# Pass 1 of a Mamba block planned with other durations, with a third x_proj tile and the last batch's splits on VectorE

## The chip, the cores and the metric

The kernel runs on one core of a Trainium2 chip. The metric is the device time of one execution in microseconds, lower is better. A core has five instruction streams that run beside each other and wait for each other by semaphores: TensorE (PE: matmuls and transposes, into PSUM), VectorE (DVE), ScalarE (ACT), GpSimd (POOL) and SyncE (SP), which here issues nearly all DMAs. Each stream runs in the order in which its instructions were written.

## The reference

The input is 8 images of 64 x 64 pixels with 96 channels. The part that matters for this case is the first layer's projections; after them come a selective scan, and an attention and a quantized feed-forward layer.

```python
xz = einsum('bhwc,ec->bhwe', groupnorm(x), in_proj_w)       # 96 -> 2 x 192
xin, z = split(xz, 2)
xc = silu(depthwise_conv3x3(xin) + conv_b)                  # 192 channels, 64 x 64
xs = stack([xc by rows, xc by columns, both reversed])      # 4 directions
x_dbl = einsum('bkdl,kcd->bkcl', xs, x_proj_weight)         # 192 -> 6 + 16 + 16
dts, Bs, Cs = split(x_dbl)
delta = softplus(dts @ dt_projs_w + bias)
h = h * exp(delta * A) + delta * u * Bs ;  y = sum_n(h * Cs)   # scan over 4096 positions, 16 states
```

Everything is computed in float32 accuracy. Bs and dts are later multiplied on TensorE in bfloat16, so each float32 value is split into three bfloat16 values that add up to it.

## The kernel before

There are three passes, one after the other, with scratch tensors in DRAM between them. `pass1` makes u (the convolved channels, in both orders), z, the x_proj result and its splits. `pass2` is the selective scan, in 192 pieces of 1024 positions. `pass3` does the rest. Passes 2 and 3 aren't edited.

**Pass 1's units of work.** Batches go in pairs. The 192 channels of a pair of batches are held as three chunks of 128 partitions: chunk 0 (128 channels of the first batch), chunk 1 (128 of the second) and chunk 2 (the other 64 of both). A batch is cut into eight groups of 512 positions. The kinds of unit are:

- `statistics(b, q)`: SP loads 512 positions of x, PE transposes them (four 128-wide transposes into a `pt` tile), VectorE takes `bn_stats`.
- `group_norm(b)`: a few tiny instructions on VectorE, PE (results `pm` and `pv`) and GpSimd give mean and inverse deviation.
- `projection(b, q)`: load and transpose again, normalize on VectorE (`xn`), three matmuls of in_proj (tiles `pa`), copied or passed through SiLU by ScalarE, z stored.
- `convolution(pair, c)`: nine taps on VectorE over 128 x 4096 elements into a tile `u`; then ScalarE applies SiLU in four pieces for the transposed order (`ut`, stored) and in two halves in place.
- `x_projection(b, o, q)`: two matmuls into a tile `px`, evicted to an SBUF tile `xd` by ScalarE (for odd q of the last pair by VectorE) and stored to `xd_d`. It needs the SiLU of chunk 2 and of the batch's own chunk to be done.
- `split(b, o, ...)`: once all eight `xd` of a batch and an order o are stored, SP loads rows of them as `bq`; ScalarE casts to bfloat16, a subtraction leaves the rest, ScalarE casts that, another subtraction gives the third part, and SP stores `bs` to `b_d` or `dt_d`. There are three of these for each batch and order, 48 in all, each with two casts and two subtractions.

**What sets the order.** The units are Python generators. Before an instruction is written, a unit yields the engine it wants, the duration it is planned with, optionally a delay after it (0.3 us if none is given), and optionally a counter of PSUM tiles (`Slots`) that must be free. `weave` keeps a planned clock for each engine and always lets the unit go on that can begin first; ties go by the order of kinds in `room`, which also limits how many units of a kind are open. So the durations in the yields take no time themselves: they decide in what order the instructions stand in each engine's stream, and on SP in what order DMAs are issued. `InOrder` keeps that order as it is written. If an instruction is reached before what it waits for is ready, all behind it on its engine wait too.

**Tiles that are shared.** [...] `p1tr` 2 tiles, `p1mm` 3, `p1px` 2 and `p1ps` 1 (for `pm` and `pv`). `xd`, `bq` and `bs` have three buffers each, `xn` and the loads of projections four.

Every line of pass 1 goes through the recording helper at line 89, which is why the profile names that line throughout; instructions are told apart by their tiles.

Of the kernel before, what the change touches and what calls it, by code (L numbers as in the profile page):

```python
# [33 lines left out]
F32 = mybir.dt.float32  # L34
# [8 lines left out]
P = 128  # L43
# [189 lines left out]
def pass1(ctx, tc, g, consts, ident, mhalf, engines, u_d, z_d, xd_d, b_d, dt_d):  # L233
# [8 lines left out]
    four = ctx.enter_context(tc.tile_pool(name="p1four", bufs=4))  # L242
    ps_tr = ctx.enter_context(tc.tile_pool(name="p1tr", bufs=2, space=PSUM))
    ps_mm = ctx.enter_context(tc.tile_pool(name="p1mm", bufs=3, space=PSUM))
    ps_px = ctx.enter_context(tc.tile_pool(name="p1px", bufs=2, space=PSUM))
    ps_one = ctx.enter_context(tc.tile_pool(name="p1ps", bufs=1, space=PSUM))
    Q = GRP // P

    ORDER = (0, 2, 1)
# [31 lines left out]
        pool.memset(t[:, 1 : HH + 1, WW + 1 : WW + 2], 0.0)  # L281

    sts, gms, us, done = {}, {}, {}, {}
    pts, mms, pxs = Slots(2), Slots(3), Slots(2)
    counts = {}

    def one_more(key, of, end):
# [14 lines left out]
    def statistics(b, q):  # L302
        if b > 1:
            yield "proj", b - 2
        yield "sp", 0.5, 2.0
        x = transposed(three, "xs", b, q)
        next(x)
        yield "pe", 0.7, 0.3, pts
        pt, slot = next(x), pts.taken
        end = yield "dve", 0.7  # L310
        if b not in sts:
            sts[b] = two.tile([C, NG, 6], F32, name="st")
        dve.bn_stats(sts[b][:, q, :], pt[0:C, :])
        pts.release(slot, end)
        one_more(("st", b), NG, end)

    def group_norm(b):

        yield "st", b
        yield "dve", 0.2  # L320
        mv = two.tile([C, 2], F32, name="mv")
        dve.bn_aggr(mv, sts[b].rearrange("p a b -> p (a b)"))
        yield "pe", 0.3
        pm = ps_one.tile([P, 2], F32, name="pm", tag="pm")
        pe.matmul(pm[0:C, 0:1], gmat, mv[:, 0:1], start=True, stop=True)
        yield "dve", 0.5
        gm = wp.tile([C, 2], F32, name=f"gm{b}")
        dve.tensor_copy(gm[:, 0:1], pm[0:C, 0:1])
        dq = two.tile([C, 1], F32, name="dq")
        dve.tensor_sub(dq, mv[:, 0:1], gm[:, 0:1])  # L330
        dve.scalar_tensor_tensor(dq, dq, dq, mv[:, 1:2], ALU.mult, ALU.add)
        yield "pe", 0.3
        pv = ps_one.tile([P, 2], F32, name="pv", tag="pm")
        pe.matmul(pv[0:C, 0:1], gmat, dq, start=True, stop=True)
        yield "dve", 0.2
        dve.tensor_copy(gm[:, 1:2], pv[0:C, 0:1])
        end = yield "pool", 1.0
        pool.tensor_scalar(gm[:, 1:2], gm[:, 1:2], 1e-5, None, ALU.add)
        pool.tensor_tensor(gm[:, 1:2], gm[:, 1:2], mhalf[0:C, 0:1], ALU.pow)
        gms[b] = gm  # L340
        done["stats", b] = end

    def projection(b, q):

        pair, j = b // 2, b % 2
        cols = slice(q * GRP, (q + 1) * GRP)
        rows = slice(1 + q * RPG, 1 + (q + 1) * RPG)
        inner = slice(1, WW + 1)
        own, other = slice(64 * j, 64 * j + 64), slice(64 - 64 * j, P - 64 * j)
        third = xpad[2 + pair % 2]  # L350
        yield "stats", b
        yield "sp", 0.5, 2.0
        x = transposed(four, "xt", b, q)
        next(x)
        if pair > 0:
            yield "conv", pair - 1, j
        if pair > 1:
            yield "conv", pair - 2, 2
        yield "pe", 0.7, 0.3, pts
        pt, slot = next(x), pts.taken  # L360
        end = yield "dve", 0.7
        pts.release(slot, end)
        xn = four.tile([C, GRP], F32, name="xn")
        dve.tensor_scalar(xn, pt[0:C, :], gms[b][:, 0:1], gms[b][:, 1:2], ALU.subtract, ALU.mult)
        def product(w):
            yield "pe", 1.1, 0.3, mms
            p = ps_mm.tile([P, GRP], F32, name="pa", tag="mm")
            pe.matmul(p, w, xn, start=True, stop=True)
            return p, mms.taken

        pa, slot = yield from product(w_in[:, 0:P])
        end = yield "act", 0.6
        act.copy(xpad[j][:, rows, inner], pa.rearrange("p (h w) -> p h w", w=WW))
        mms.release(slot, end)
        pa, slot = yield from product(w_mix[:, j, :])
        yield "act", 0.6
        act.copy(third[own, rows, inner], pa[own, :].rearrange("p (h w) -> p h w", w=WW))
        z1 = three.tile([P, GRP], F32, name="z1")
        end = yield "act", 0.6
        act.activation(z1[other, :], pa[other, :], AF.Silu)  # L380
        one_more(("proj", b), NG, end)
        mms.release(slot, end)
        pa, slot = yield from product(w_in[:, DI : DI + P])
        z0 = three.tile([P, GRP], F32, name="z0")
        end = yield "act", 0.6
        act.activation(z0, pa, AF.Silu)
        mms.release(slot, end)
        yield "sp", 0.9
        sp.dma_start(z_d[b][P:DI, cols], z1[other, :])
        sp.dma_start(z_d[b][0:P, cols], z0)  # L390

    def convolution(pair, c):

        ty = c // 2
        src = xpad[c + pair % 2 if c == 2 else c]
        for b in [2 * pair, 2 * pair + 1] if c == 2 else [2 * pair + c]:
            yield "proj", b
        before = {0: (pair - 1, 1), 2: (pair, 0), 1: (pair, 2)}[c]
        at = 3 * pair + ORDER.index(c) - UB
        if at >= 0:  # L400
            old, c_old = at // 3, ORDER[at % 3]
            for b in {0: (2 * old,), 1: (2 * old + 1,), 2: (2 * old, 2 * old + 1)}[c_old]:
                yield "xproj", b
            yield "stored", old, c_old
        if before[0] >= 0:
            yield "conv", *before
        u = None
        for tap in range(9):
            end = yield "dve", 2.6 if tap == 0 else 4.4, 0.0
            if tap == 0:  # L410
                u = us_p.tile([P, L], F32, name="u")
                us[pair, c] = u
                uv = u.rearrange("p (h w) -> p h w", w=WW)
            win = src[:, tap // 3 : tap // 3 + HH, tap % 3 : tap % 3 + WW]
            if tap == 0:
                dve.tensor_scalar(uv, win, conv_w[:, ty, tap : tap + 1], None, ALU.mult)
            else:
                dve.scalar_tensor_tensor(uv, win, conv_w[:, ty, tap : tap + 1], uv, ALU.mult, ALU.add)
        done["conv", pair, c] = end
        if before[0] >= 0:  # L420
            yield "stored", *before
        parts = chunk_rows(pair, c)
        for w in (slice(i, i + WW // 4) for i in range(0, WW, WW // 4)):
            yield "act", 1.2
            ut = two.tile([P, L // 4], F32, name="ut")
            act.activation(ut.rearrange("p (w h) -> p h w", h=HH), uv[:, :, w], AF.Silu, bias=conv_b[:, ty, :])
            yield "sp", 0.5
            for part, b, ch in parts:
                sp.dma_start(u_d[b][1][ch, w.start * HH : w.stop * HH], ut[part, :])
        for h in range(2):  # L430
            cols = slice(h * (L // 2), (h + 1) * (L // 2))
            end = yield "act", 1.9
            act.activation(u[:, cols], u[:, cols], AF.Silu, bias=conv_b[:, ty, :])
        done["u", pair, c] = end
        end = yield "sp", 0.5
        for part, b, ch in parts:
            sp.dma_start(u_d[b][0][ch, :], u[part, :])
        done["stored", pair, c] = end

    def x_projection(b, o, q):  # L440
# [3 lines left out]
        yield "u", pair, 2  # L444
        px = None
        for ty, u, part in ((0, us[pair, j], slice(0, P)), (1, us[pair, 2], half)):
            end = yield ("pe", 0.85) if px else ("pe", 0.85, 0.3, pxs)
            if px is None:
                px, slot = ps_px.tile([P, GRP], F32, name="px", tag="px"), pxs.taken
            if o == 0:  # L450
# [4 lines left out]
        one_more(("xproj", b), 2 * NG, end)  # L455
        by_dve = pair == NB // 2 - 1 and q % 2 == 1
        end = yield ("dve" if by_dve else "act"), 0.6
        xd = three.tile([2 * NXD, GRP], F32, name="xd")
        (dve.tensor_copy if by_dve else act.copy)(xd, px[0 : 2 * NXD, :])
        pxs.release(slot, end)  # L460
        end = yield "sp", 0.5, 2.5
        sp.dma_start(xd_d[b][o][:, q * GRP : (q + 1) * GRP], xd)
        one_more(("xd", b, o), NG, end)

    def split(b, o, row, rows, pieces, at, dst):

        wide, used = GRP, rows * pieces
        yield "xd", b, o
        yield "sp", 0.5, 2.5
        bq = three.tile([P, wide], F32, name="bq")  # L470
        src = xd_d[b][o][row : row + rows].rearrange("r (s t) -> (r s) t", s=pieces)
        sp.dma_start(bq[0:used], src[:, at : at + wide])
        yield "act", 0.6
        bs = three.tile([P, NS, wide], BF16, name="bs")
        act.copy(bs[0:used, 0, :], bq[0:used])
        yield "pool", 1.2
        pool.tensor_sub(bq[0:used], bq[0:used], bs[0:used, 0, :])
        yield "act", 0.6
        act.copy(bs[0:used, 1, :], bq[0:used])
        yield "pool", 1.2  # L480
        pool.tensor_sub(bs[0:used, 2, :], bq[0:used], bs[0:used, 1, :])
        yield "sp", 0.9
        half = used // 2
        for k2 in range(2):
# [612 lines left out]
```

## Time and profile before

The three timed runs took 10697.7, 10700.71 and 10703.4 us; the profiled execution has a span of 10692.9 us (its run 10694.64 us).

| | busy us of the whole span | busy us in the first 1000 us |
|---|---|---|
| PE matmuls | 7776.9 | 723.2 |
| VectorE | 9619.3 | 595.8 |
| ScalarE | 9298.7 | 429.5 |
| GpSimd | 9181.8 | 259.8 |

The first pass's last split is stored at 954 us of the span, and the second pass's first matmul begins at 975 us. Groups of the first pass in the trace:

| instruction | count | mean |
|---|---|---|
| VectorE conv tap, 128 x 4096 | 96 | 4.59 us |
| PE px record, 128 x 76, 512 columns (a matmul is two records) | 256 | 0.944 us |
| PE pa record, 96 x 128, 512 columns (two to a matmul) | 256 | 0.712 us |
| GpSimd subtraction `bq<-bq,bs`, 128 x 512 | 32 | 2.36 us |
| ScalarE cast `bs<-bq`, 128 x 512 | 64 | 0.618 us |
| ScalarE SiLU piece `ut`, 128 x 1024 | 48 | 2.08 us |
| ScalarE copy `xd<-px`, 76 x 512 | 112 | 0.583 us |

How to read the lines shown below: in the list of waits, "A <- B: total, times, longest" says that engine and tile A stood idle until B was done. In the timeline a line has start, duration (or the stretch of several merged instructions), engine, operation, out<-in tiles, shape, count, and in brackets the idle time of that engine before it and what ended it. "SPq" is SP issuing DMAs.

### The profile page before, as it was taken

To read this page: it belongs to the slowest core of one execution; us is meant where nothing else is said; L and a number is where in the kernel's file an instruction comes from. 1 tells how busy PE (TensorE), PEld (TensorE's weight loads), DVE (VectorE), ACT (ScalarE), POOL (GpSimd) and SP (SyncE) were. 2 spreads that over 40 slices of the span, in tenths; PEclk is the share of its full clock that TensorE was granted. 3 is DMA by queue.
4 is the path that set the end of the run, shared out by engine and by line. 5 is a ranking of instruction groups with operands and counts; after the bars stand their busy time and mean duration, and the time that the engine had idled before them with its cause. 6 is when DMAs were issued, how large, how long until landed. Compare 5 with 4: busy or idle time off the path is not lost.

```text
span 10692.9 us, 151366 instructions
## 1 busy us (share of the span) xinstructions
PE 7776.9 (73%) x51232; PEld 6178.1 (58%) x51232; DVE 9619.3 (90%) x6982; ACT 9298.7 (87%) x21355; POOL 9181.8 (86%) x3270
## 2 busy tenths in 40 slices
PE   6876777777767777777777777777777777766887
PEld 3222656666656666665656666665565666655766
DVE  6664999999999999999999999999999999997776
ACT  4445999999999999999999999999999999996665
POOL 1324999999999999999999999999999999997886
PEclk8777999998899999999899999988999999897776
DMA  5555666669896666689976766789766667997442
GB/s 145 170 165 168 211 217 216 210 211 204 197 210 215 210 219 213 213 205 203 200 218 210 222 211 214 208 200 204 216 210 215 217 207 214 199 198 184 135 128 59
DMA packets 928009, 2103.22 MB, mean 197 GB/s; under 512 B 274391, under 2 KB 422648, under 8 KB 925700
## 3 DMA queue, kind: packets, MB, share of 16 engines
q1 hardware_dynamic: 919812, 2092.79, 69.6%
q8 instruction: 410, 6.72, 0.3%
q14 instruction: 363, 2.97, 0.1%
q10 hardware_dynamic: 7424, 0.74, 0.1%
HBM read 1917.59 MB, written 175.66 MB: 196 GB/s over the span
## 4 chain that ended last, share of the span: by engine, by line
ACT 28%; DVE 20%; PE 17%; issue 17%; POOL 13%; DMA 4%; SPq 1%; ACTq 0%; DVEq 0%; POOLq 0%
DVE h L89 15%; ACT x L89 13%; ACT da L89 10%; POOL c L89 9%; PE wide L89 6%; PE acc L89 6%; DVE wide L89 3%; PE px L89 2%; PE mm L89 2%; ACT L89 1%; POOL xg L89 1%; PE pa L89 1%; ACT delta L89 1%; DMA xdt<-dt_d 1%; SPq L89 1%
## 5 line engine op out<-in xcount | busy, mean ns | idle before, releaser
L89 POOL TENSOR_TENSOR c<-c,h 128x2048 f32<-128x2048 f32 x1536 | 6965.6, 4549 | 395.8 <-DVE h L89 335.4
L89 DVE TENSOR_TENSOR_SCAN h<-da,carry,wide 128x1024 f32<-128x1024 f32 x2304 | 5253.5, 2331 | 204.4 <-PE wide L89 147.4
L89 ACT ACTIVATE x<-duT,bT 128x128 f32<-128x128 f32 (+1 forms) x14336 | 4155.2, 366 | 63.5 <-PE wide L89 57.5
L89 PE MATMUL acc<-ident,c 128*128 128x128 f32 x24576 | 3480.5, 297 | 546.6 <-POOL c L89 539.6
L89 ACT ACTIVATE da<-delta,a_neg 128x1024 f32<-128x1024 f32 x3072 | 3504.2, 1144 | 345.6 <-DVE h L89 333.9
L89 PEld LDWEIGHTS acc<-ident,c 128*128 128x128 f32 x24576 | 3133.3, 155 | 881.1 <-POOL c L89 747.9
L89 PE MATMUL wide<-ident,x 128*128 128x128 f32 x11264 | 1614.0, 292 | 877.9 <-DVE h L89 861.0
L89 PEld LDWEIGHTS wide<-ident,x 128*128 128x128 f32 x11264 | 1344.9, 149 | 1171.7 <-DVE h L89 509.3
L89 DVE TENSOR_TENSOR_SCAN h<-da,wide 128x1024 f32<-128x1024 f32 x768 | 1707.0, 2270 | 82.8 <-PE wide L89 62.0
L89 DVE TENSOR_TENSOR wide<-du,wide 128x1024 f32<-128x1024 f32 x1216 | 1459.2, 1212 | 156.9 <-PE wide L89 156.8
L89 PE MATMUL wide<-xb,sel 96*128 96x512 bf16 x2432 | 752.4, 394 | 584.9 <-DVE h L89 494.7
L89 POOL TENSOR_TENSOR xg<-duT,bT 128x512 f32<-128x512 f32 (+1 forms) x640 | 891.4, 1408 | 82.3 <-PE wide L89 65.1
L89 PE MATMUL wide<-ident,xg 128*128 128x128 f32 x3584 | 500.2, 285 | 239.6 <-DVE h L89 233.7
L89 PEld LDWEIGHTS <-sel 96*128 96x128 bf16 x2432 | 223.0, 101 | 776.0 <-DVE h L89 387.3
L89 PEld LDWEIGHTS wide<-ident,xg 128*128 128x128 f32 x3584 | 412.6, 146 | 316.0 <-issue 143.9
L89 POOL TENSOR_TENSOR du<-delta,u 128x1024 f32<-128x1024 f32 x192 | 455.0, 2370 | 101.4 <-ACT delta L89 92.2
L89 ACT ACT_TABLE_LOAD x385 | 494.0, 1283 | 6.8
L89 PE MATMUL px<-u,w_xp 128*76 128x512 f32 (+1 forms) x512 | 409.5, 929 | 76.5 <-ACT xd L89 47.8
L89 POOL TENSOR_TENSOR bq<-bq,bs 128x512 f32<-128x512 f32 (+1 forms) x48 | 114.2, 2392 | 401.3 <-ACT bs L89 401.2
L89 DVE SCALAR_TENSOR_TENSOR u<-xpad,conv_w,u 128x4096 f32<-128x4096 f32 x96 | 440.6, 4590 | 1.2
L89 PEld LDWEIGHTS px<-u,w_xp 128*76 128x76 f32 (+1 forms) x512 | 78.8, 190 | 364.4 <-issue 217.2
L89 ACT COPY xd<-px 76x512 f32<-76x512 f32 x112 | 65.2, 583 | 254.8 <-PE px L89 169.9
(130 smaller groups left out, 6224.0 us busy)
## 6 DMA issues: line engine op xcount, KB each, us to landing
c<-xd_d SPq DMA_DIRECT2D x1024, 1024.0 KB
c<-xd_d SPq DMA_DIRECT2D x1024, 512.0 KB
u<-u_d SPq DMA_DIRECT2D x128, 512.0 KB
xdt<-dt_d SPq DMA_DIRECT2D x1152, 36.0 KB
xb<-b_d SPq DMA_DIRECT2D x384, 96.0 KB
u<-u_d SPq DMA_DIRECT2D x128, 256.0 KB
y_d<-y SPq DMA_DIRECT2D x24, 1024.0 KB
y<-y_d SPq DMA_DIRECT2D x64, 384.0 KB
```

Source lines behind the costliest of these rows:

```text
L89: ins = getattr(self.engine, op)(*args, **kwargs).ins
```

## The change

Durations and delays in the yields are replaced in many places: x loads (0.5 with 2.0 to 0.6 with 4.0), `pa` products (1.1 to 0.75, delay 0.3 to 0.4), SiLU pieces (1.2 to 2.1), x_proj matmuls (0.85 to 0.9, delay to 0.4), xd stores (0.5 with 2.5 to 0.9 with 3.0), `bq` loads (0.5 with 2.5 to 0.7 with 4.0), and the subtractions of `split`, planned at 1.2 before and now at 4.4 for batches 0 to 5 and 2.5 for batch 6. For batch 7 the subtractions are given to VectorE and planned at 0.65. x_proj gets a third PSUM tile and a fourth `xd` buffer. The bank comes from `pm` and `pv`, which now take tiles of the projections' pool and wait for a free one. Counting the built instructions, only the twelve subtractions of batch 7 change engine; the order changes on all five streams within pass 1, and passes 2 and 3 keep theirs.

```diff
-    ps_px = ctx.enter_context(tc.tile_pool(name="p1px", bufs=2, space=PSUM))
-    ps_one = ctx.enter_context(tc.tile_pool(name="p1ps", bufs=1, space=PSUM))
+    ps_px = ctx.enter_context(tc.tile_pool(name="p1px", bufs=3, space=PSUM))
...
-    pts, mms, pxs = Slots(2), Slots(3), Slots(2)
+    pts, mms, pxs = Slots(2), Slots(3), Slots(3)
...
-        yield "sp", 0.5, 2.0
+        yield "sp", 0.6, 4.0
...
-        yield "pe", 0.3
-        pm = ps_one.tile([P, 2], F32, name="pm", tag="pm")
+        yield "pe", 0.3, 0.3, mms
+        pm, slot = ps_mm.tile([P, GRP], F32, name="pm", tag="mm"), mms.taken
         pe.matmul(pm[0:C, 0:1], gmat, mv[:, 0:1], start=True, stop=True)
-        yield "dve", 0.5
+        end = yield "dve", 0.5
+        mms.release(slot, end)
...
-        end = yield "dve", 0.7
+        end = yield "dve", 0.8
...
-            yield "pe", 1.1, 0.3, mms
+            yield "pe", 0.75, 0.4, mms
...
-            yield "act", 1.2
+            yield "act", 2.1
...
-            end = yield "act", 1.9
+            end = yield "act", 2.0
...
-            end = yield ("pe", 0.85) if px else ("pe", 0.85, 0.3, pxs)
+            end = yield ("pe", 0.9, 0.4) if px else ("pe", 0.9, 0.4, pxs)
...
-        xd = three.tile([2 * NXD, GRP], F32, name="xd")
+        xd = four.tile([2 * NXD, GRP], F32, name="xd")
...
-        end = yield "sp", 0.5, 2.5
+        end = yield "sp", 0.9, 3.0
...
+        name, cost, by = ("dve", 0.65, dve) if b == NB - 1 else ("pool", 4.4 if b < NB - 2 else 2.5, pool)
         yield "xd", b, o
-        yield "sp", 0.5, 2.5
+        yield "sp", 0.7, 4.0
...
-        yield "pool", 1.2
-        pool.tensor_sub(bq[0:used], bq[0:used], bs[0:used, 0, :])
+        yield name, cost
+        by.tensor_sub(bq[0:used], bq[0:used], bs[0:used, 0, :])
         yield "act", 0.6
         act.copy(bs[0:used, 1, :], bq[0:used])
-        yield "pool", 1.2
-        pool.tensor_sub(bs[0:used, 2, :], bq[0:used], bs[0:used, 1, :])
+        yield name, cost
+        by.tensor_sub(bs[0:used, 2, :], bq[0:used], bs[0:used, 1, :])
```

More of the change, by code (lines that the diff above doesn't have):

```diff
@@ L331, in group_norm @@
         dve.scalar_tensor_tensor(dq, dq, dq, mv[:, 1:2], ALU.mult, ALU.add)
-        yield "pe", 0.3
-        pv = ps_one.tile([P, 2], F32, name="pv", tag="pm")
+        yield "pe", 0.3, 0.3, mms
+        pv, slot = ps_mm.tile([P, GRP], F32, name="pv", tag="mm"), mms.taken
         pe.matmul(pv[0:C, 0:1], gmat, dq, start=True, stop=True)
-        yield "dve", 0.2
+        end = yield "dve", 0.2
+        mms.release(slot, end)
         dve.tensor_copy(gm[:, 1:2], pv[0:C, 0:1])
@@ L351, in projection @@
         yield "stats", b
-        yield "sp", 0.5, 2.0
+        yield "sp", 0.6, 4.0
         x = transposed(four, "xt", b, q)
```

## The prediction

> **What bounds the kernel now.** I read the busy share by slice first. Slices 5 to 36 stand at 9 for VectorE, ScalarE and GpSimd (the second pass); only the first four slices are loose. I then split the first 1000 us into windows of 40 us (columns: stretch, length, busy us with instructions of PE, weight loads, VectorE, ScalarE, GpSimd, then granted PE clock, DMA share, GB/s).
>
> ```profile
> DVE  6664999999999999999999999999999999997776
> PEclk8777999998899999999899999988999999897776
> ...
> 400.00:440.00 40.00, 29.54 (x35) 6.14 (x34) 39.68 (x13) 9.97 (x16) 30.86 (x7) 0.55 0.43 111
> 440.00:480.00 40.00, 37.11 (x46) 8.05 (x45) 9.19 (x5) 12.37 (x17) 13.04 (x8) 0.50 0.43 128
> 480.00:520.00 40.00, 24.49 (x55) 10.51 (x53) 28.48 (x11) 24.33 (x34) 13.94 (x6) 0.76 0.63 203
> 640.00:680.00 40.00, 32.11 (x34) 5.56 (x34) 17.01 (x4) 9.49 (x17) 24.92 (x10) 0.50 0.32 90
> 800.00:840.00 40.00, 13.06 (x17) 2.79 (x16) 19.12 (x5) 16.37 (x14) 15.19 (x6) 0.57 0.59 153
> ```
>
> The first pass ends near 954 us (last split stored); PE begins the second pass at 974.96. In 440-480 VectorE worked 9 us of 40 and PE 37, at half clock; in 800-840 nobody worked half of the time. So no engine bounds the first pass as a whole: orders written out by the planner make engines wait in turn. Next the waits over 0-960 (who, for whom: us, times, longest):
>
> ```profile
> DVE xn L89 <- PE pt L89: 156.0, 32, 31.1
> PEld px L89 <- ACT xd L89: 92.5, 42, 9.8
> ACT bs L89 <- DMA bq<-xd_d: 55.3, 18, 9.7
> ACT bs L89 <- POOL bq L89: 52.7, 19, 8.7
> PE px L89 <- ACT xd L89: 47.8, 14, 9.0
> ACT xd L89 <- DMA xd_d<-xd: 45.8, 10, 8.1
> ...
> SPq L89 <- POOL bs L89: 100.2, 18, 14.4
> ```
>
> Read upward: SP stands 100 us in front of stores of `bs` that GpSimd has not made; xd stores queue behind; ScalarE can't evict px or is stuck in a cast; PE waits for px; VectorE waits for the transposes behind px. The timeline shows one whole instance, batches 3 and 4:
>
> ```profile
> 614.22 0.58 ACT L89 COPY xd<-px 76x512 f32<-76x512 f32 x1 [3.25 <-PE px L89]
> 630.66 1.76 ACT L89 CAST bs<-bq 128x512 bf16<-128x512 f32 x3 [9.73 <-DMA bq<-xd_d]
> 632.95 7.73 PE L89 MATMUL px<-u,w_xp 128*76 128x512 f32 x8 [8.95 <-ACT xd L89]
> 639.08 0.62 ACT L89 CAST bs<-bq 128x512 bf16<-128x512 f32 x1 [4.20 <-POOL bq L89]
> 644.30 13.80 POOL L89 TENSOR_TENSOR bs<-bq,bs 128x512 bf16<-128x512 f32 x3
> 645.52 15.40 PE L89 MATMUL px<-u,w_xp 128*76 128x512 f32 x16 [4.83 <-ACT xd L89]
> 663.98 23.07 PE L89 MATMUL px<-u,w_xp 128*76 128x512 f32 x24 [3.06 <-ACT xd L89]
> 688.18 1.59 DVE L89 TENSOR_SCALAR xn<-pt,gm 96x512 f32<-96x512 f32 x2 [31.10 <-PE pt L89]
> ```
>
> One float32 px matmul is two records: 24 records in 23.07 us are 12 matmuls of 1.92 us. VectorE lost 31.1 us at 688 because projection 7's transposes stand behind all of batch 4's px. The same shape, with 30.8 us, ends at 476 (batch 2).
>
> [...] a GpSimd split subtraction takes 1.15 us with VectorE idle (945 us) and 5.33 beside taps (705 us). The old plan charged 1.2 for all. [...] The pools take 2+3+2+1 before and 2+3+3 after; no run here shows a limit. [...] px matmuls are issued without a gap from 664 to 687 and the clock stays 0.50. I don't count on a faster clock. [...] the trace has no such VectorE row (nearest: the xd copy, 0.687).
>
> **The change part by part.** Per-engine work is the same but for 12 subtractions; what moves is the order on every queue of the first pass. Passes two and three keep theirs, and SP's list at the seam (last bq loads, two c loads, last stores, xdt) is the same. So I follow the order from stretch to stretch.
>
> *Batch 2, from the last px of batch 1 (401.7) to projection 5's first transposes (476): 74 us.* Before, statistics of batch 6 preceded conv (pair 1, chunk 1); now its 8 transposes and `bn_stats` lie between the taps. PE sheds 8 x 0.9 = 7 us ahead of batch 1's end. But px of batch 2 now follow those transposes, which come at the pace of taps: about four pairs of tap and two statistics, 4 x (4.47+1.4) = 24 us. Projection 5's transposes stand ahead of 5 of the 32 px matmuls, so 27 x 1.72 (half clock, 46 us) precede them: 24+46 = 70 instead of 74. With the 7 us: 11. The waits for ScalarE inside the old stretch (6.28+4.18+2.77 = 13.2) are in this sum. Beside projection 5 PE was busy 24.5 of 40 us, so the 5 moved matmuls (9 us) fit; the cast wait behind GpSimd near 490 (4.5) goes. Take -15.
>
> *Batch 4, from 614.2 to 688: 74 us.* The new ScalarE order puts two first casts of batch 3's last splits ahead of the last two SiLU pieces of conv (2,2), which px needs. They wait for the store and bq load: cast at 630.66 before; some 10 us after the last px now, as no xd stores of batch 4 are ahead on SP. So PE starts px 10+1.2+4 = 15 us late, a new wait: the SiLU pieces are queued behind the casts on ScalarE, PE waits for them, and px heads its queue. From there no px eviction stands in front of a GpSimd result not yet due, so the 8.95+4.83+3.06 = 16.8 us go. Ahead of projection 7's transposes are now 25 matmuls (7 of 32 follow): 15 + 25 x 1.72 = 58 us, 16 less than 74. Behind it, conv (3,0) took 688 to 746 for 8 taps and 7 or 8 xn (42 us of VectorE), with PE waiting 4.5 and 8.5 us for ScalarE stuck in casts (701, 712). PE now has 7 px (12 us) and eight projections (30 to 38): about 50 instead of 58. Take -24.
>
> *Start to 370.* In 281-342 PE waited 4.4+2.8+7.6+6.4 = 21 us for loads of x on SP, whose head is often a `bs` store. Later stores and a planned landing of 4 us relieve some: -5, between 0 and -15.
>
> *Last pair.* PE stood 26.3 us (to 826) for conv (3,2)'s SiLU. ScalarE, after the last px of batch 5 (796), waited 6.5 for bq, 3.2 and 2.7 for GpSimd, with four casts ahead of the first piece; now one cast is ahead: 803.7 + four SiLU pieces (8.2) + two halves (4.0) + four casts (2.4) = 818 instead of 828: -10. The third px tile and fourth xd tile let PE run past 2.1-us SiLU pieces and xd stores (gaps 3.9, 4.9, 4.7): -5.
>
> *Last splits on VectorE.* VectorE has 12 x 0.69 = 8.3 us more where it is mostly idle (2 us busy in 920-960). At the very end six subtractions at 1.15 become 0.69; loads land at 944.7 to 947.4, and load, cast, sub, cast, sub ends about 951 instead of 953.9: -3 (-1 to -5).
>
> *Costs.* pm and pv of the group norm now hold a product tile until VectorE copies them, up to one tap (4.47). Only norms 1 and 3 fall among products: 4 x 4.47 = 18 at most, 0 at least; take +3. Products planned at 0.75 and px at 0.9 while half clock makes them 1.7: new misorderings, 0 to +30; I take +10. GpSimd's queue has norms 5 and 7 behind subtractions, but projections 5 and 7 come over 30 us later: 0.
>
> Sum: -15-24-5-10-5-3+3+10 = -49; I keep 5 of it back, as ends of stretches are estimates: -44. The profiled span is 10692.9 (its run 10694.6); the three timed runs have median 10700.7, some 8 above the span. 10692.9-44+8 = 10657.
>
> **Rivals.** (a) *The PE clock rises.* Half clock covers 429-494 and 637-702. If px runs without gaps at full clock, 40 of those 52 matmuls drop from 1.72 to 0.86: 34 us more, 10615. For: 910-927 was mostly at full clock. Against: the gapless trains at 452 and 664 were not. (b) *Hidden.* The new waits at the SiLU gates and the px matmuls moved behind projections take the gain back: PE has 708 of the first 960 us, and px at half clock fills what is freed. Then only tail and last splits remain, 5 to 20 us: 10690. (c) *Slower, through GpSimd.* The plan packs 72 subtractions at 4.4 back to back (12 in a row beside conv (1,2) and (1,1)). If most take the 5.33 of the trace or more, each runs 0.93 us late, b_d stores again block SP, and x loads and xd stores pile up: 72 x 0.93 = 67 us. Against: 75 of the 96 took 3.5 us or less before (mean 2.21). It cancels the gain where two thirds of it are exposed, and loses over 0.2% where all of it is: 10725 and up. (d) That the order does not change is excluded by the built instruction lists.
>
> **How the numbers follow.** Chances: forecast 0.50 (own range 10637 to 10678), (a) 0.17, (b) 0.22, (c) 0.11. 0.2% is 21 us, about what a measurement of this kernel can tell from no change. Faster beyond it: the first two, 0.67; within: (b), 0.22; slower: 0.11. The range runs from inside (a) to inside (b): 10605 leaves out some 0.06 below and 10712 some 0.13 above.
>
> **What would show it.** Right: the wait of SP for GpSimd's bs well under 100 us; ScalarE casts waiting for GpSimd under 25 of the 52.7; no VectorE wait of 30 us for projections 5 and 7; second pass's first matmul near 930 instead of 975; 12 VectorE subtractions near 0.69 us. Wrong: that matmul at 965 or later with PE waits for ScalarE's u grown (b); subtractions at 5.3 throughout and SP still waiting for bs (c); PE clock above 0.8 in px stretches (a). A difference after the seam would refute my claim that the second pass is only shifted.

## The result, and the profile after

The changed kernel took 10582.95 us (median of four runs, 10577.81 to 10595.03), against 10702.06 us for the kernel before on the same chip (four runs, 10697.7 to 10720.15): a ratio of 0.9887, 95% interval 0.9870 to 0.9904. That is 119 us less, where the forecast was 44 less; 10583 lies below the range. The spans of the two profiled executions are 10692.9 and 10583.4 us.

All of it comes from the first pass. The first matmul of the second pass moved from 974.96 to 860.0 us (-115.0), and what follows it took 9717.9 us before and 9723.4 after (+5.5, inside the spread of 9710 to 9729 that this unedited part shows in the profiles of all the kernels below). In the page, the loose part at the left is shorter than in the row of before, and the rest of the row is the same nines:

```profile
DVE  7767999999999999999999999999999999997776
```

The work of PE in the first pass is the same 1440 matmul records. These are the windows that hold them, the first of before, the second of after (columns as above: stretch, length, busy us with instructions of PE, weight loads, VectorE, ScalarE, GpSimd, then PE clock, DMA share, GB/s):

```profile
0.00:955.00 955.00, 707.83 (x1440) 232.31 (x1440) 579.30 (x305) 404.96 (x539) 244.62 (x134) 0.74 0.54 160
0.00:840.00 840.00, 666.52 (x1440) 220.72 (x1440) 598.01 (x317) 404.57 (x539) 301.71 (x122) 0.81 0.61 181
```

Up to the second pass PE was busy 707.8 us and is now busy 666.5: 41 us less for the same records, at a mean clock of 0.81 instead of 0.74 (22 us of it in the `pa` products, from 222.2 to 199.9 us, and 11 in px, from 409.5 to 398.1). The rest, 115 - 41 = 74 us, is time in which PE stood idle before and does not now. VectorE, ScalarE and GpSimd work as long or longer (GpSimd 57 us longer). So the gain is in waits and in PE's clock, and no engine got less to do. This is an account of PE's time; whether the clock rose because the waits went is not shown by it.

By stage, with the names of the forecast (a milestone's time before and after, and the change of the stretch that ends there):

| stretch ends with | before | after | change | forecast |
|---|---|---|---|---|
| conv (1,2) | 369.1 | 343.8 | -25.3 | -5 |
| last px of batch 1 | 401.7 | 356.5 | -19.9 | (in the next) |
| projection 5's first `xn` | 476.0 | 416.3 | -14.5 | -15, with the row above |
| last px of batch 3 | 614.2 | 533.8 | -20.7 | 0 |
| projection 7's first `xn` | 688.2 | 589.5 | -18.3 | -16 |
| conv (3,0) | 746.0 | 637.5 | -9.8 | -8 |
| last px of all | 938.4 | 822.9 | -7.0 | -15 |
| first matmul of pass 2 | 974.96 | 860.0 | +0.5 | -3 |
| costs and reserve | | | | +18 |
| sum | | | -115.0 | -44 |

The waits of after up to 880 us, with the lines that answer to those of before, and one line of before that was not shown:

```profile
DVE xn L89 <- PE pt L89: 67.4, 25, 10.5
...
PE px L89 <- ACT u L89: 39.2, 3, 23.0
ACT bs L89 <- DMA bq<-xd_d: 36.9, 13, 10.1
PE pt L89 <- DMA xt<-in_x: 16.7, 7, 4.9
...
ACT bs L89 <- POOL bq L89: 11.7, 4, 4.5
...
SPq L89 <- POOL bs L89: 8.7, 6, 4.4
```

```profile
PE pt L89 <- DMA xt<-in_x: 56.2, 18, 7.6
```

SP waits for GpSimd's `bs` 8.7 us instead of 100.2, and ScalarE's casts wait for GpSimd 11.7 instead of 52.7. PE waits for the projections' x loads 16.7 instead of 56.2, a line that the prediction looked at only between 281 and 342 us. VectorE's longest wait for transposes is 10.5 us, not 31.1. One of these lines grew: PE's wait for ScalarE's `u` (27.2 before).

Where the forecast of the stages was low, PE's idle time and its clock say why. The two mixed stretches, in which x_proj and projections take turns, first both of before, then both of after:

```profile
225.00:402.00 177.00, 150.07 (x335) 52.09 (x333) 111.20 (x67) 91.90 (x124) 51.43 (x22) 0.82 0.60 182
476.00:614.00 138.00, 115.68 (x256) 42.48 (x254) 93.32 (x47) 83.31 (x108) 21.61 (x14) 0.77 0.64 197
```

```profile
225.00:357.00 132.00, 124.73 (x285) 41.41 (x284) 95.91 (x46) 83.48 (x117) 55.14 (x16) 0.90 0.66 207
416.00:534.00 118.00, 111.11 (x266) 37.44 (x264) 95.77 (x43) 79.11 (x113) 64.32 (x17) 0.94 0.69 215
```

PE idled 26.9 and 22.3 us there, and now 7.3 and 6.9. In the second, which holds nearly the same records, 10 records more take 4.6 us less, at clock 0.94. The list of waits of before, cut to these two windows, has PE waiting for `xt` 21.7 and 16.5 us: 38 of the 49 us idle.

The stretch of batch 4, which the prediction worked out by steps, is this in the timeline of after:

```profile
548.80 5.61 PE L89 MATMUL px<-u,w_xp 64*76 64x512 f32 x6 [9.81 <-ACT u L89]
556.83 31.68 PE L89 MATMUL px<-u,w_xp 128*76 128x512 f32 x40 [2.42 <-ACT xd L89]
589.48 1.59 DVE L89 TENSOR_SCALAR xn<-pt,gm 96x512 f32<-96x512 f32 x2 [10.47 <-PE pt L89]
```

PE takes up px for good at 548.80, 15.0 us after batch 3's last px: the new wait for the SiLU pieces behind the casts, at the size forecast. From there 46 px records come almost without a gap, and VectorE's wait ahead of projection 7 is 10.47 us instead of 31.10.

### The profile page after: what moved, and what is told of

Same layout as the page of the kernel before. It is cut to its first block, busy times and chain, and to the rows that moved or that the text cites. A ratio compares the mean times of both kernels' runs of the same rounds, so it can differ in the third digit from the quotient of the medians.

```text
span 10583.4 us, 151357 instructions
## 1 busy us (share of the span) xinstructions
PE 7747.7 (73%) x51232; PEld 6175.5 (58%) x51232; DVE 9636.1 (91%) x6994; ACT 9299.0 (88%) x21355; POOL 9239.9 (87%) x3258
## 4 chain that ended last, share of the span: by engine, by line
ACT 29%; DVE 21%; PE 18%; issue 17%; POOL 12%; DMA 2%; SPq 1%; ACTq 0%; DVEq 0%; POOLq 0%
DVE h L89 15%; ACT x L89 13%; ACT da L89 10%; POOL c L89 8%; PE wide L89 6%; PE acc L89 5%; DVE wide L89 3%; PE px L89 3%; PE mm L89 2%; ACT L89 1%; PE pa L89 1%; POOL xg L89 1%; ACT delta L89 1%; ACT duT L89 1%; DVE u L89 1%
## 5 line engine op out<-in xcount | busy, mean ns | idle before, releaser
L89 PE MATMUL wide<-ident,x 128*128 128x128 f32 x11264 | 1615.5, 292 | 877.8 <-DVE h L89 862.7
L89 PE MATMUL px<-u,w_xp 64*76 64x512 f32 (+1 forms) x512 | 398.1, 910 | 46.6 <-ACT u L89 39.2
L89 PE MATMUL mm<-w_out,gt 128*128 128x96 f32 (+1 forms) x1024 | 261.9, 376 | 37.9 <-POOL gt L89 16.5
L89 PEld LDWEIGHTS px<-u,w_xp 64*76 64x76 f32 (+1 forms) x512 | 76.4, 177 | 315.4 <-issue 227.1
```

What stands on the lines that cost most here:

```text
L89: ins = getattr(self.engine, op)(*args, **kwargs).ins
```

## The experiments

The theory after this comparison: a planned duration that is too small puts an instruction ahead of its data in a stream that keeps its written order, and all behind it waits (SP stood 100.2 us in front of `bs` before); the largest part is the subtractions on GpSimd, planned at 1.2. The rivals: the x loads' longer planned landing; the third px tile; truer durations of PE and ScalarE; the last splits on VectorE. Every plan is computed anew by the scheduler, so each edit moves many instructions. Times are medians, and the 95% interval of a ratio reaches some 15 us to either side for most runs; "pass 2 at" is the second pass's first matmul in the profile.

### One part taken out of the changed kernel

**`u_pool`**: GpSimd's subtractions planned at 1.2 again (batch 7 stays on VectorE).

```diff
-        ... else ("pool", 4.4 if b < NB - 2 else 2.5, pool)
+        ... else ("pool", 1.2, pool)
```

> The changed kernel with one number put back: GpSimd's split subtractions are planned at 1.2 us for batches 0 to 6 (batch 7 stays on VectorE). Split theory (most of the gain is that casts, xd copies and stores no longer stand behind subtractions that aren't ready): SP's wait for bs on GpSimd goes from 8.7 us back over 60, the second pass's first matmul from 860 to 910 or later, time 10640 or more. Tile theory (the third px tile is most of it): under 15 us lost, 10585 to 10600. Load theory (the x loads' planned landing is most of it): under 15 us lost.

Measured: 10673.75 us, ratio to before 0.9976 [0.9965, 0.9987]; pass 2 at 950.1. GpSimd's planned durations alone take back 91 of the 119 us. SP's wait up to 960 us, and the instruction in its timeline with PE's longest wait:

```profile
SPq L89 <- POOL bs L89: 134.8, 23, 16.8
```

```profile
799.53 9.01 PE L89 MATMUL px<-u,w_xp 64*76 64x512 f32 x12 [47.17 <-ACT u L89]
```

SP stands in front of unmade `bs` again, longer than before the change (100.2). The lag builds up by stages: against the changed kernel the end of conv (1,2) is the same (343.9 and 343.8), the last px of batches 1, 3, 4 and of all are 14, 51, 70 and 90 us later. In the last pair, PE waits 47.17 us for conv (3,2)'s SiLU where it waited 22.98 with the change.

**`u_xload`**: the x loads' durations of before.

```diff
-        yield "sp", 0.6, 4.0      (statistics and projection)
+        yield "sp", 0.5, 2.0
```

> The changed kernel with x loads planned as before (0.5 us, landing 2.0 later). Split theory: 5 to 20 us lost, at the loads of x between 240 and 370 us. Load theory: 35 us or more lost, PE waits for x loads back from 28 us over 70.

Measured: 10605.55 us, 0.9911 [0.9897, 0.9926]; pass 2 at 878.1: 23 us lost, though its interval overlaps that of the change. PE's wait for `xt` is 21.3 us, not the 56.2 of before, even under the old load times. That the splits are out of SP's way doesn't account for this: they are in `o_pool_b` too, below, and there the wait is 41.5. Which other edits of the change keep it low is not shown.

**`u_px2`**: two px tiles, and `pm` and `pv` back in their own pool.

```diff
-    ps_px = ... bufs=3 ...            pxs = Slots(3)
+    ps_px = ... bufs=2 ...            pxs = Slots(2)
+    ps_one = ctx.enter_context(tc.tile_pool(name="p1ps", bufs=1, space=PSUM))
-        yield "pe", 0.3, 0.3, mms
-        pm, slot = ps_mm.tile(...), mms.taken
+        yield "pe", 0.3
+        pm = ps_one.tile(...)             (pv alike)
```

> The changed kernel with two px tiles again and pm and pv in a bank of their own; all durations as changed. Split theory: 5 to 20 us lost, 10590 to 10605, PE waits for xd copies grow from 39 us but not to 92. Tile theory: over 50 us lost, 10635 or more.

Measured: 10584.54 us, 0.9891 [0.9876, 0.9906]; pass 2 at 865.6: no difference from the change (0.9887) that can be told. PE's waits for an evicted px do grow, to 20.1 us from 7.5, and batch 3's last px is 16 us later; but the last px of all is only 6 later, and the end is not later within what can be measured. The fourth `xd` tile stayed in; no run takes it out.

**`u_lastpool`**: batch 7's subtractions on GpSimd, planned at 2.5.

```diff
-        name, cost, by = ("dve", 0.65, dve) if b == NB - 1 else (...)
+        name, cost, by = ("pool", 4.4 if b < NB - 2 else 2.5, pool)
```

> The changed kernel with batch 7's splits on GpSimd, planned at 2.5. All theories: 0 to 5 us lost, at the seam only (first matmul of the second pass at 860 to 865); the first 800 us differ by nothing but order.

Measured: 10586.06 us, 0.9894 [0.9877, 0.9910]; pass 2 at 862.6. Three us, inside the uncertainty. The subtractions themselves cost what was forecast, from the changed kernel's view by tile (lowest, median and highest ns, then from when to when):

```profile
L89 DVE TENSOR_TENSOR bq<-bq,bs x6: 678/684/693, 816.3 to 833.9; 128x512 f32<-128x512 f32 x4, 96x512 f32<-96x512 f32 x2
```

0.684 us on VectorE agrees with the 0.69 that the forecast took. The nearest row that it had in the trace of before is VectorE's copy of `xd`, 0.687 us.

**`u_peact_b`**: PE's and ScalarE's durations of before, and VectorE's of `xn`.

```diff
-            yield "pe", 0.75, 0.4, mms
+            yield "pe", 1.1, 0.3, mms
-            ... ("pe", 0.9, 0.4, pxs)
+            ... ("pe", 0.85, 0.3, pxs)
-            yield "act", 2.1
+            yield "act", 1.2
-            end = yield "act", 2.0
+            end = yield "act", 1.9
-        end = yield "dve", 0.8
+        end = yield "dve", 0.7
```

> The changed kernel with the planned durations of PE's products and px, of ScalarE's SiLU pieces and of xn put back (1.1, 0.85, 1.2, 1.9, 0.7). Split theory: within 15 us of the changed kernel, since the gain sits in the split. If SiLU pieces at 2.1 are needed too: 20 us or more lost, with the wait of PE for u grown at 549 and 707.

Measured: 10608.78 us, 0.9910 [0.9895, 0.9925]; pass 2 at 879.1: 26 us lost. PE's wait for `u` did not grow with it (34.8 us, 39.2 with the change), so nothing shows that it was lost at the SiLU pieces. Two more runs took this apart. **`u_pe`** (only the two edits of PE's durations):

> The changed kernel with only PE's planned durations put back (products 1.1 with 0.3, px 0.85 with 0.3). Together with ScalarE's and VectorE's they were worth 26 us, ScalarE's alone about 10. If the rest is PE's: 10 to 20 us lost, 10593 to 10603. If the order is only shuffled: within 10 us.

Measured: 10598.14 us, 0.9899 [0.9885, 0.9914]; pass 2 at 884.5, 24 later: 15 lost. **`u_ut`** (only ScalarE's two):

> The changed kernel with only ScalarE's SiLU durations put back (1.2 and 1.9 for 2.1 and 2.0). The five durations of PE, ScalarE and VectorE together were worth 26 us. If SiLU pieces carry them: 15 us or more lost, 10600 or later. If PE's do: under 10 us lost.

Measured: 10592.92 us (10569.85 to 10596.44), 0.9895 [0.9880, 0.9910], pass 2 at 852.8. The median is 10 slower, the profiled execution 15 faster (10568.1): unclear.

**`u_spsplit_b`**: SP's durations in x_proj and split of before.

```diff
-        end = yield "sp", 0.9, 3.0      (store of xd)
+        end = yield "sp", 0.5, 2.5
-        yield "sp", 0.7, 4.0            (load of bq)
+        yield "sp", 0.5, 2.5
```

> The changed kernel with the durations of xd stores and bq loads put back (0.5 with 2.5 for both). Split theory: GpSimd's 4.4 carries it, under 15 us lost. Rival: the landing of stores and loads is the part of the split that matters for ScalarE's casts: 25 us or more lost, ScalarE's wait for bq grown from 37 us over 60.

Measured: 10595.57 us, 0.9896 [0.9882, 0.9911]; pass 2 at 867.6: 13 lost, at the edge of what can be told. ScalarE's wait for `bq` is 55.0 us (36.9 with the change, 55.3 before): the line that this edit sets, and `v_bq8`, below, shows that taking most of it away gains nothing.

### One part put alone into the kernel before

**`o_pool_b`**: only GpSimd's planned durations.

```diff
-        yield "pool", 1.2                              (both)
+        yield "pool", 4.4 if b < NB - 2 else 2.5
```

> The kernel before with one number changed: GpSimd's split subtractions planned at 4.4 us for batches 0 to 5 and 2.5 for 6 and 7; tiles, engines and all other durations as before. Split theory: most of the 91 us that the opposite edit lost come here too, 10610 to 10650, SP's wait for bs on GpSimd below 30 us. If the number works only together with the other durations (an order that fits by luck): 10670 or more.

Measured: 10642.33 us, 0.9942 [0.9925, 0.9959]; pass 2 at 922.5: alone it gains 60 us. In the waits up to 960 us:

```profile
DVE xn L89 <- PE pt L89: 101.4, 28, 22.1
...
PE pt L89 <- DMA xt<-in_x: 41.5, 15, 7.1
...
SPq L89 <- POOL bs L89: 12.5, 8, 4.4
```

SP's wait for `bs` is gone with this one edit (100.2 before), and VectorE's wait for transposes is past halfway (156.0 before, 67.4 with the whole change). But PE still waits 41.5 us for x loads, of 56.2 before: most of that wait was not behind the `bs` stores.

**`o_xload_b`**: only the x loads' durations.

```diff
-        yield "sp", 0.5, 2.0      (statistics and projection)
+        yield "sp", 0.6, 4.0
```

> The kernel before with x loads planned at 0.6 us with a landing 4.0 later, all else as before. Split theory: 0 to 20 us gained, 10680 to 10700. If load and split durations are independent and add: about 20 gained, as the opposite edit lost.

Measured: 10686.77 us (20 runs), 0.9984 [0.9977, 0.9990]; pass 2 at 956.9: 16 us gained. Its waits:

```profile
PE pt L89 <- DMA xt<-in_x: 26.1, 11, 7.0
...
SPq L89 <- POOL bs L89: 105.5, 16, 17.8
```

PE's wait for `xt` falls by 30 us and half of that reaches the end, while SP stands in front of `bs` as before. So this wait answers more to the place of the loads in SP's own list than to the `bs` stores.

**`o_poolx`**: both edits.

> The kernel before with two edits of the change: GpSimd's subtractions planned at 4.4 and 2.5, and x loads at 0.6 with 4.0. Alone they gave 60 and 16 us. If they are independent: 76 us, 10623 to 10632. If both free the same wait (SP's queue ahead of x loads): no more than the larger, about 10640.

Measured: 10637.3 us, 0.9930 [0.9915, 0.9945] (before in this comparison: 10706.6); pass 2 at 908.6. The gain of 69 lies under the sum of the two alone, 76. In the profiles, pass 2 begins 66 us earlier, and 52 + 18 = 70 would be the sum. So they add up nearly, and about 50 us of the change are still missing. PE's wait for `xt` is 11.3 us with both.

### Variations of the changed kernel

**`v_pool55`**: 4.4 becomes 5.5.

> The changed kernel with GpSimd's subtractions planned at 5.5 instead of 4.4 for batches 0 to 5 (5.3 to 6.1 is what they take beside conv taps). If the plan must only be late enough (split theory): within 15 us of 10583. If the gain is an order that happens to fit 4.4: 25 us or more lost.

Measured: 10591.03 us, 0.9897 [0.9882, 0.9912], pass 2 at 859.6. The exact figure doesn't matter once it is late enough.

**`v_bq8`**: a planned landing of 8 instead of 4 us for `bq`, so that the first casts come later on ScalarE.

```diff
-        yield "sp", 0.7, 4.0
+        yield "sp", 0.7, 8.0
```

> The changed kernel with bq loads planned to land 8 us after issue instead of 4. ScalarE waits 37 us in casts for bq in the changed kernel, 10.1 of it ahead of the SiLU that lets px of batch 6 start. If these waits are on the path: 10 to 20 us gained, ScalarE's wait for bq under 20 us. If splits only come later and px waits elsewhere: within 10 us, or up to 10 lost at the end, where the last splits are bare.

Measured: 10591.53 us, 0.9897 [0.9883, 0.9912]; pass 2 at 858.0. Its waits:

```profile
PE px L89 <- ACT u L89: 44.4, 4, 30.1
ACT bs L89 <- DMA bq<-xd_d: 9.2, 4, 5.5
...
SPq L89 <- POOL bs L89: 41.8, 15, 6.7
```

ScalarE waits 9.2 us for `bq` instead of 36.9, and PE's wait for SiLU does not shrink (39.2): the wait moved, and SP again waits for `bs`.

**`v_px14`** and **`v_px17`**: x_proj matmuls planned at 1.4 and at 1.7 instead of 0.9, as the traces have them at 0.94 to 1.92 us. **`v_pa11px14`**: 1.4, and `pa` at 1.1.

```diff
-            ("pe", 0.9, 0.4, pxs)
+            ("pe", 1.4, 0.4, pxs)          (1.7 in v_px17)
```

> The changed kernel with px matmuls planned at 1.4 us (the traces have 0.86 at full clock and 1.72 at half) instead of 0.9. If truer durations help further: 10 to 20 us gained, 10563 to 10573, because conv (3,2)'s SiLU comes before the first cast of batch 5's last splits and the 23 us wait of PE for u shrinks. If order has no more to give, px at half clock being the bound: within 10 us.

> The changed kernel with px planned at 1.7 us, the duration at half clock; 1.4 gained 29. If the truer number wins by placing other work before px: within 10 us of the kernel with 1.4, 10545 to 10565. If 1.4 was a lucky order: back at 10575 or more.

> The changed kernel with px planned at 1.4 and products at 1.1 with a delay of 0.4 (traces: 0.86 at full clock, more at half). If PE's planned durations should all be true: 10540 to 10555. If the product's number does not matter: within 10 us of the kernel with px at 1.4.

Measured: `v_px14` 10553.77 us (10547.14 to 10563.54), 0.9861 [0.9845, 0.9878], pass 2 at 834.3; `v_px17` 10576.9, 0.9875 [0.9858, 0.9891], pass 2 at 858.8; `v_pa11px14` 10602.32, 0.9899 [0.9884, 0.9913], pass 2 at 877.8. The first is the fastest version here, by 29 us against the change. The stages place the gain: 12 us between batch 1's last px and projection 5, and 12 in the last pair, where PE waits 17.7 us for `u`.

With the change a px matmul takes 1.55 us on average (398.1 us for 256 matmuls of two records) and a `pa` 1.04 (199.9 for 192). So 1.4 and 1.7 lie equally near to the measured mean and differ by 23 us (24 by the start of pass 2, though the intervals of the two ratios overlap), and 1.1 for `pa` is nearer to it than 0.75 and costs 49. That a duration nearer to the truth makes a better order doesn't hold at this size: part of the gain of 1.4 looks like an order that happens to fit.

### What the runs say together

Every variation that leaves GpSimd's planned durations near the measured ones lies between 10554 and 10609 us, and begins pass 2 between 834.3 and 884.5 (860.0 with the change): small edits of durations move the time by some 20 us either way, whether they are nearer to the measured durations or farther off. Outside lie only GpSimd at 1.2 (10674) and the plans with most of the old durations (10637 to 10702). So the late subtractions are settled as the main cause (60 us alone, 91 when undone). The x loads' landing comes second (16 alone, clear of zero with 20 runs, and 23 when undone); that is no larger than what small edits do, and it is put down to the loads because the wait for them falls with it. The remaining parts measure 26 (PE and ScalarE), 13 (`xd` and `bq`) and 3 (last splits) as undone. With 60 + 16 that makes 118 of the 119, but this closeness is chance: when all are taken as undone the sum is 91 + 23 + 26 + 13 + 3 + 2 = 158. How much of the 26 and 13 is a truer duration and how much a lucky order, these runs can't tell.

## Why the prediction was wrong in size

**The mechanism held.** The forecast read SP's wait for `bs` as the root, and what follows from it: px evictions and casts stuck on ScalarE, transposes stuck behind px. For these it was right; for the x loads only in small part, as is told below. SP's wait fell to 8.7 us, the casts' to 11.7 (under 25 was the mark), the waits of 30 us ahead of projections 5 and 7 are 9.1 and 10.47, and `u_pool` and `o_pool_b` show the cause by undoing it and by doing it alone. The second pass is only shifted, to within 5.5 us.

**Batch 4** was forecast at -24, and measured -18.3 - 9.8 = -28. Each step is found: PE late by 15.0 us (15), 55.7 us to projection 7 (58), 48 for conv (3,0) behind it (50).

**The step that failed is "Start to 370: -5".** It measured -25.3 up to conv (1,2), and -20 more to batch 1's last px, of which the forecast had only the 7 us of the moved transposes. The step saw the right wait (21 us of PE for x loads) and then took a quarter of it. Nothing in the profile supported that: PE's idle time in 225-402 was 26.9 us, and 19.6 of it went. The cause that it named, a `bs` store at SP's head, was one of two. Either cure alone already brings most of the first 25: conv (1,2) ends at 350.9 in `o_pool_b` and at 354.4 in `o_xload_b`, 18 and 15 us earlier than before, and in `u_pool`, where the loads are planned late and SP waits 134.8 us for `bs`, it ends as with the change. Both together (`o_poolx`) bring batch 1's last px to 377.4, 24 of the 45 us. Of the rest, 22 go again when only PE's planned durations are put back (378.1 in `u_pe`), and these the forecast had entered as a cost.

**The same wait is missing a second time.** From projection 5 to batch 3's last px the sum has no term; it measured -20.7. I had priced the two stretches with a 31-us wait in them and taken the mixed stretches between as unchanged, because their waits were short. They were many: 18 for `xt` in all, 56.2 us. The wait is the same as one pair earlier, but not its cause. In this stretch, first before, then in `o_pool_b`:

```profile
PE pt L89 <- DMA xt<-in_x: 16.5, 5, 5.5
SPq L89 <- POOL bs L89: 12.8, 1, 12.8
```

```profile
PE pt L89 <- DMA xt<-in_x: 16.9, 5, 6.4
SPq L89 <- POOL bs L89: 3.1, 2, 2.4
```

With the `bs` stores off SP's head PE waits for x loads as long as before, and the stretch is only 1.2 us shorter. With the loads planned late alone (`o_xload_b`) that wait is 7.3 us, but PE now waits 11.5 for ScalarE's z, and the stretch is 1.4 shorter. Both edits together bring 11.0; the other ten come with the rest of the change.

Beside these two entries (20 and 21 us short), the rows up to projection 5 are 19 short and batch 4's two 4; the last pair and the seam were taken 8 and 3.5 too well; and the costs and the reserve, 18, did not show. Together these make the 71 us between -44 and -115.

**The rise of the clock was put in a rival.** Rival (a), 10615, expected the full clock in trains of px. (Its half-clock stretches are 418 to 482 and 626 to 691 in the trace, 11 us earlier than it says.) That came in part: batch 2's px (378 to 431) ran at 0.89 and batch 4's (535 to 611) at 0.72, where they had 0.52 and 0.55, but the last pair's ran at 0.50 from 708 to 726. Where px and projections are mixed and PE no longer waits, the clock rose from 0.82 to 0.90 and from 0.77 to 0.94 in the windows shown. PE's busy time up to the second pass fell 41 us, of which the forecast counted nothing. The forecast went by two px trains of before, from 452 and from 664 on, which ran without a gap at 0.50. Gapless px trains do run higher at times, from 0.50 to 0.76 in the windows of the last section, and the mixed stretches have 0.90 and 0.94. So "I don't count on a faster clock" left out a real term. Neither the forecast nor the rival saw that the clock matters for only half of the px matmuls, those of order 0 (0.94 us at full clock and 1.81 at half, where order 1 has 1.78 and 1.81); the last section shows that too. The forecast took 1.72 us for every px matmul at half clock; the train of 24 records that it works out at 1.92 is all of order 1.

**The costs of +13 and the reserve of +5** were not paid, as far as the stages show. Norms waiting for a product tile are part of `u_px2`, which makes no difference. Planning px at 1.4 gains 29 us more, so orders better than the change's exist; but the kernel before planned px as short (0.85), so this was no new cost. Taken together PE's new durations look like a gain, not a cost (15 us lost in `u_pe`, 24 by the start of pass 2).

**The tail was forecast too well.** The last pair has -7.0 for -15: the new order still puts a cast that waits 10 us for `bq` in front of the SiLU, and PE's wait for conv (3,2) fell from 26.3 to 22.98 us, not by 10. The third px tile (-5, with the fourth `xd` tile, which no run takes out) and the last splits (-3) show nothing that can be told from zero (`u_px2`, `u_lastpool`).

**Rival (c)**, slower through GpSimd, was right in its premise and wrong in its result. The subtractions did get slower, from a mean of 2.20 to 3.09 us with a highest of 6.19, as 58 of 84 now run beside taps and 30 of 96 did. Before, none of the 66 without a tap beside it took over 1.18 us, and the 30 beside taps took 4.49 on average; with the change none of the 26 without a tap took over 1.17, and the 58 beside taps took 3.95. The traces show that the two go together, not the reason. But with the consumers placed later too, ScalarE and SP together wait only 20 us for them. **Rival (b)**, hidden, fell: the wait at the SiLU gates grew by 12 us in all (27.2 to 39.2) and paid back little.

## What to carry to other kernels

When several waits are to go, price every stretch in which a victim waits, by the total of its waits (here 56 us for `xt` in 18 pieces), and not only the stretches with one long wait. And don't put a victim's wait down to the one blocker that you have seen ahead of it: taking the `bs` stores off SP's head left 41.5 of these 56 us, planning the loads themselves later left 26.1, and both left 11.3. In a planned order, give an engine the duration that it has beside the others' work, or more (a subtraction beside taps took 4.49 us before, and at most 1.18 away from them): a microsecond too late cost nothing here that can be told (5.5 for 4.4), and 1.2 where 2.2 to 3.1 was measured cost 60 to 90 us of the first 975. And compare several nearby plans before crediting an edit with 20 us: that much comes and goes with the order alone.

## What was not expected of the hardware

**Half of the px matmuls take nearly the same time at full and at half clock.** x_projection reads `u` by rows for order 0 and by columns (neighbours 64 elements apart) for order 1; the weights differ too, shapes and types are the same. These are px records of batches 2 and 6 of the changed kernel (lowest, median and highest ns, then from when to when): order 0 at full clock and at half, then order 1 at full clock and at half.

```profile
L89 PE MATMUL px<-u,w_xp x24: 589/592/653, 383.7 to 394.8; 64*76 64x512 f32 x12, 128*76 128x512 f32 x12
L89 PE MATMUL px<-u,w_xp x19: 1054/1061/1136, 708.1 to 725.2; 64*76 64x512 f32 x11, 128*76 128x512 f32 x8
L89 PE MATMUL px<-u,w_xp x7: 1030/1033/1057, 396.7 to 402.0; 64*76 64x512 f32 x4, 128*76 128x512 f32 x3
L89 PE MATMUL px<-u,w_xp x13: 1033/1043/1134, 739.4 to 750.3; 128*76 128x512 f32 x8, 64*76 64x512 f32 x5
```

Where nothing lies between them, records start 0.43 to 0.52 us apart in the first line and 0.85 to 0.99 in the others. So a px matmul of order 0 takes 0.94 us at full clock and 1.81 at half, and one of order 1 takes 1.78 at full clock, 1.81 at half, and 1.92 in the half-clock trains of before: there half clock cost 2 to 8 per cent. That the reading by columns is the reason fits the kernel, but is not shown: no run changes it alone.

**A gapless px train can keep half clock for long.** In the changed kernel PE's clock was full for 65 us at a stretch twice, while PE took transposes, projections and px in turn with hardly a gap. The first of these, two stretches of the changed kernel with px almost alone, and one of `o_pool_b`:

```profile
276.00:342.00 66.00, 64.23 (x171) 22.97 (x170) 50.33 (x26) 45.77 (x67) 25.90 (x8) 1.00 0.77 237
649.00:684.00 35.00, 35.00 (x44) 6.51 (x42) 34.75 (x8) 17.46 (x22) 14.55 (x4) 0.76 0.62 203
708.00:726.00 18.00, 17.35 (x20) 3.61 (x18) 14.16 (x5) 4.30 (x7) 11.76 (x4) 0.50 0.75 197
395.00:446.00 51.00, 51.00 (x54) 8.96 (x54) 30.48 (x7) 11.63 (x21) 22.24 (x7) 0.50 0.32 92
```

PE is over 96% busy in all four. The second follows other work without a gap; ahead of the third PE had stood idle for 23 us, and ahead of the fourth for 6. So px alone doesn't settle the clock (0.76 in the second, 0.50 in the third and fourth), and it was 0.50 through the 51 us of busy PE in the fourth. What does decide it, the mix, the order or the idle time ahead, no run here was made to tell.
